# A ring of half batches that two stages of a fused graph kernel share

## The chip, the cores and the metric

The kernel runs on one core of a Trainium2 chip. The metric is the device time of one execution in microseconds, the median of three runs. A profile is one further execution, recorded by the hardware profiler; its span runs from the first to the last instruction. Engines are named as in the profile: PE (matrix products), DVE (vector), ACT (activations), POOL (GpSimd) and SP (here it only issues DMAs; SPq is its queue of issues).

## The reference, cut to what matters

Four graph layers are applied to `x` of 128 batches x 128 nodes x 128 features with an adjacency of 128 x 128 per batch. The second layer is the one that costs:

```python
# layer 1, h is the normed and rectified x
D = jnp.abs(x[:, :, None, :] - x[:, None, :, :])      # every pair of nodes
h = jnp.einsum('bijc,oc->bijo', D, W1) + b1            # 128 -> 64 features per pair
m = jnp.mean(h, axis=(0, 1, 2))                        # over ALL batches and pairs
v = jnp.mean((h - m) ** 2, axis=(0, 1, 2))
h = (h - m) / jnp.sqrt(v + EPS) * g1 + be1
h = _leaky(h)
s = jnp.einsum('bijo,uo->biju', h, W2)[..., 0] + b2[0]
s = jnp.where(A_init > 0, s, NEG)
A = jax.nn.softmax(s, axis=-1)
y = jnp.einsum('bij,bjc->bic', A, x)
y = y @ Wg.T + bg                                      # then a second norm over all batches
```

The mean and the variance `m`, `v` are taken over all batches, so the pair features of every batch have to exist before the first score can be computed. They don't fit on the core: 2 MB for each of 128 batches (pairs are symmetric, so only about half of them are made). A second norm over all batches (`mg`, `vg`) stands before the rest of the layer and the two attention layers that follow.

## The kernel before

It has three stages, cut by the two norms over all batches. The batches go in 32 groups of four (`G = 4`, `NG = 32`).

**First stage** (L261 to L740). For every batch four tiles `t` are made (`NT = 4`), each of 128 x 1024 elements. Per tile: a difference (`d`, L311, on DVE for two tiles and on POOL for two), its absolute value (L352, ACT, three tiles of four), the products with W1 into PSUM (`hp`, L321 and L324, PE), a copy to SBUF (`evacuate`, L335, ACT), and the statistics of the copy (L342, L343, DVE). The copies of one batch stand in one tile `halves[b]` of four parts (`hs`, three buffers, 16 KB per partition each). When the fourth part is there, one DMA of 2 MB writes it to memory, `HP[b]` (L370). Beside this runs the first graph layer of each group (`chain`, L401). The order of all this is set ahead of time: every piece is a `step` with an engine, a cost, the steps it comes after and a rank, and `_ordered` (L115) writes the instructions of each engine in the order of a small plan. SP is one of these engines, so its DMAs stand in one queue, in which a DMA that waits holds those behind it.

**The seam** (L743 to L780). From the statistics `ST1` come, in a few small steps on DVE, PE and POOL in a pool `bn`, the factors `scale1` and `bias1`.

**Second stage** (L783 to L1108). The pair features come back in halves of 1 MB: `fetch(n)` loads the n-th half into a tile `z` (L796), of which there are `FETCHED = 10`. Ten loads are issued ahead; slot `b` then issues two more (L903, L904), into the buffers that batch `b` leaves. A slot (`slot`, L871) does for batch `b + 1` the activation of the first half in place (L878, ACT), the rectified second half into `zr` (L882, ACT) and the leaky maximum of the first (L896, DVE); for batch `b` the products with W2 (`products`, L849: `w2z` with the first half, `w2l` with the second, `w2r` with `zr`); and for batch `b - 1` the copy `su` (L874), the turn into rows `pk` (L860) and the scores `sk` (L867). After each fourth batch a `chain` (L907) is worked through for the group, with its pieces hung into later slots by `at(slot, place, work)`: the scores are written to memory (`rows`, L928), x is loaded (L931), the scores are read back in another order (`u`, L935), then come eight slots of softmax and small products, from `s0 = 4 g + 9` on, up to `y` (L978) and its statistics (`stored`, L980). `x1` and `y` go to memory (L983, L984), but for the last five groups (`KEPT = 5`), which stay on chip in `X1` and `Y`. After the last batch, 12 slots hold only the last groups' chains, and besides them `brief` (L1018), small constants for the third stage, from slot 129 on.

**Third stage** (L1111 to L1400). From the second norm's statistics (`ST2`) come `scale2` and `bias2`; then the rest of the layer and two attention layers per group, planned by `_planned` (L79), with the groups in `Y` first.

Tiles come from pools. A pool that takes memory which another pool has given back lets its first user wait for all that was done in that memory. In the kernel before, the first `fetch` therefore waits for the first stage's buffers and for the pool `bn` of the seam.

Of the kernel before, what the change touches and what calls it, by code (L numbers as in the profile page):

```python
# [17 lines left out]
P = 128  # L18
G = 4
# [149 lines left out]
def tile_gnn_stack(ctx: ExitStack, tc: tile.TileContext, a: dict, out: bass.AP):  # L169
# [5 lines left out]
    res = ctx.enter_context(tc.tile_pool(name="res", bufs=1))  # L175
    small = ctx.enter_context(tc.tile_pool(name="small", bufs=4))
    early = ctx.enter_context(ExitStack())
    psum = early.enter_context(tc.tile_pool(name="psum", bufs=1, space=bass.MemoryType.PSUM))
    banks = {"sm": 2}

# [80 lines left out]
    with tc.tile_pool(name="c0", bufs=1) as c0, tc.tile_pool(name="p0", bufs=2) as p0, ExitStack() as ctx0:  # L261
# [33 lines left out]
        def step(name, engine, cost, after, rank, work, takes=(), gives=()):  # L295
            steps.append((name, engine, cost, after, takes, gives, rank, work))
# [31 lines left out]
        def evacuate(i):  # L328

            b, t = divmod(i, NT)  # L330
            if t == 0:
                halves[b] = p0.tile([P, NT, KC * P], F32, name="hs", bufs=3)
                if b % G == 0:
                    stats[b // G] = p0.tile([P, 2 * NT + 1, G, 6], F32, name="st")
            nc.scalar.copy(halves[b][:, t, :], linear.pop(i))  # L335

        def statistics(i):

            b, t = divmod(i, NT)
            last = t == NT - 1  # L340
            hs, st = halves[b][:, t, :], stats[b // G][:, :, b % G, :]
            nc.vector.bn_stats(st[:, 2 * t, :], hs[:, 0:512])  # L342
            nc.vector.bn_stats(st[:, 2 * t + 1, :], hs[:, 512:1024 - P * last])  # L343
            if last:
                nc.vector.bn_stats(st[:, 2 * NT, :], hs[:, 1024 - P:])
            if last and b % G == G - 1:
                of_all = stats.pop(b // G).rearrange("p a g b -> p a (g b)")
                nc.vector.bn_aggr(ST1[:, b // G, 0, :], of_all[:, 0:2 * NT, :].rearrange("p a b -> p (a b)"))
                nc.vector.bn_aggr(ST1[:, b // G, 1, :], of_all[:, 2 * NT, :])
# [4 lines left out]
        def pairs(i):  # L354

            b, t = divmod(i, NT)
            n, by_max = b // 2, t == BY_MAX
            engine, cost, rank = ("Pool", 4.22, i - 3) if t in ON_POOL else ("DVE", 2.2, i - 2)
            step(("d", i), engine, cost, [("again", n), ("d", i - 2), ("hp", i - 4)], rank, lambda: difference(i))
            if not by_max:  # L360
                step(("abs", i), "ACT", 1.8, [("d", i)], i - 1, lambda: absolute(i))
            step(("hp", i), "PE", 3.44 if by_max else 1.72,
                 [("d" if by_max else "abs", i), ("hp", i - 1), ("hs", i - 2)] + [("xw", n)] * by_max,
                 i, lambda: products(i))
            step(("hs", i), "ACT", 0.9, [("hp", i), ("hs", i - 1)]
                 + [("st", i - 2 * NT - 1), ("out", b - 3)] * (t == 0), i + 1, lambda: evacuate(i))
            step(("st", i), "DVE", (1.3 if b % G < G - 1 else 2.4) if t == NT - 1 else 1.21, [("hs", i), ("st", i - 1)], i + 2,
                 lambda: statistics(i))
            if t == NT - 1:
                step(("out", b), "SP", 0.4, [("hs", i)], i + 1.5, lambda: nc.sync.dma_start(HP[b], halves[b]))  # L370

        def features(g, half):

# [313 lines left out]

        pick = const.tile([P, 2, 8], F32, name="pick")  # L690
        nc.gpsimd.tensor_copy(pick.rearrange("p h (a c) -> p h a c", a=2),
                              ident.rearrange("p (c r) -> p r c", c=4)[:, 0:4, :]
# [12 lines left out]
                chain(g)  # L705
        for i in range(NT * NB):
            pairs(i)
        with tc.manual_schedule():

            b1 = col("b1", a["b1"], 64)  # L710
# [72 lines left out]
    early.close()  # L783
    middle = ctx.enter_context(ExitStack())
    keep = ctx.enter_context(tc.tile_pool(name="keep", bufs=1))
    Y, X1 = ({g: keep.tile([P, G, P], F32, name=f"{n}{g}") for g in range(NG - KEPT, NG)} for n in ("y", "x1"))
    psum = middle.enter_context(tc.tile_pool(name="psum2", bufs=1, space=bass.MemoryType.PSUM))
    banks = {"ps": 3, "pk": 2, "sm": 3}
    with tc.tile_pool(name="c1", bufs=1) as c1, tc.tile_pool(name="p1", bufs=2) as p1:
        fetched, prepared, scored = [], {}, {}  # L790

        def fetch(n):

            if n < 2 * NB:
                z = p1.tile([P, NT // 2 * KC * P], F32, name="z", bufs=FETCHED)
                nc.sync.dma_start(z, HP[n // 2][:, n % 2 * NT // 2:(n % 2 + 1) * NT // 2, :]  # L796
                                  .rearrange("p a b -> p (a b)"))
                fetched.append(z)

        for n in range(FETCHED):  # L800
            fetch(n)


        z0 = c1.tile([P, 1], F32, name="z0")
        nc.vector.scalar_tensor_tensor(z0, bias1, 0.01, bias1, op0=OP.mult, op1=OP.max)
# [36 lines left out]
        def at(slot, place, work):  # L842
            jobs.setdefault((slot, place), []).append(work)
# [60 lines left out]
                fetch(2 * b + FETCHED + 1)  # L904
            now(b, "s")

        def chain(g):  # L907

            rows = slots[g % 2]
            t = {}  # L910
            s0 = G * g + 2 * G + 1

            def four(out, left, right):
                for k in range(G):
# [11 lines left out]
            def to_rows():  # L926
                to = rows[0, 0, 0:1]
                nc.sync.dma_start(bass.AP(tensor=to.tensor, offset=to.offset,  # L928
                                          ap=[[ROW + 1, P], [P * ROW, G], [1, 1 + 2 * KH]]), sk[g % 2])
                t["x"] = p1.tile([P, G, P], F32, name="x", bufs=3)  # L930
                nc.sync.dma_start(t["x"], X[g])  # L931

# [50 lines left out]
                    nc.sync.dma_start(X[g], t["x1"])  # L983
                    nc.sync.dma_start(Z[g], t["y"])  # L984

            at(s0 - 4, "s", to_rows)
            at(s0 - 2, "s", from_rows)
            at(s0, "e", normed)
            at(s0, "p", lambda: turned("pt", t["h"]))
            at(s0, "l", folded)  # L990
# [25 lines left out]
        own_k = const.tile([P, 4], F32, name="own_k")  # L1016

        def brief():  # L1018
            t, end = {}, NB + 1

            def scratch():
                left = p1.tile([P, NT // 2 * KC * P], F32, tag="zr", bufs=3, name="brief")
                for name, n in (("wt0", P), ("wt1", P), ("add_b", 8), ("bounds", 24), ("square", 16), ("bound", 1),
                                ("left", P + 8), ("part", P + 8), ("one0", P + 8), ("one1", P + 8),
                                ("one2", P + 8), ("by_batch", 16)):
                    t[name], left = left[:, 0:n], left[:, n:]
                nc.gpsimd.memset(t["bounds"], 0.0)
                nc.gpsimd.memset(t["part"], 0.0)
                nc.gpsimd.memset(ones3, 1.0)
                nc.vector.tensor_copy(ident_b, ident)  # L1030
                nc.vector.tensor_scalar(no_edge, ident, NEG_EDGE, None, op0=OP.mult)
# [69 lines left out]
            at(end + 8, "l", owners)  # L1101

        with tc.manual_schedule():
            for g in range(NG):
                chain(g)
            brief()
            for b in range(-1, NB + 3 * G + 1):
                slot(b)  # L1108
# [10 lines left out]


    middle.close()
    with tc.If(nc.values_load(bounded, min_val=0, max_val=1) > 0) as cmp, \
            tc.tile_pool(name="p3", bufs=1) as p3, \
            tc.tile_pool(name="ps3", bufs=1, space=bass.MemoryType.PSUM) as ps3:
        pieces = {}
        for heads in (4, 1):
            pieces[heads] = []
# [474 lines left out]
```

## Time and profile before

| | us |
|---|---|
| runs (three) | 2803.29, 2803.65, 2803.67 |
| median | 2803.65 |
| span of the profiled execution | 2798.6 |
| first stage, to the last evacuation | 0 to 1527.6 |
| second stage, ACT's first step of a batch: first and last start | 1539.2, 2286.2 |
| last statistics of y, first step of the third stage | 2335.7, 2339.1 |

How the page is read: its first part gives each engine's busy time and share of the span, the second the span in 40 slices of 70 us with a digit for the busy tenths. Over the whole span PE is busy for 88%, DVE for 88%, ACT for 85%, POOL for 61%. An average over three stages with different limits doesn't say which of them bounds which stage. The groups of instructions that the change touches or leans on, with count, busy time, the mean duration of one in ns, and the engine's idle time before them with what ended it:

```profile
L335 ACT COPY hs<-hp 128x1024 f32<-128x1024 f32 x512 | 516.7, 1028 | 30.7 <-PE hp L324 24.0
L896 DVE SCALAR_TENSOR_TENSOR z<-z 128x2048 f32<-128x2048 f32 x128 | 295.1, 2306 | 21.7 <-ACT z L878 21.7
L878 ACT ACTIVATE z<-z,bias,scale 128x2048 f32<-128x2048 f32 x128 | 267.3, 2088 | 19.0 <-DMA z<-hp 19.0
L882 ACT ACTIVATE zr<-z,bias,scale 128x2048 f32<-128x2048 f32 x128 | 267.4, 2089 | 4.7 <-DMA z<-hp 3.8
...
hp<-hs SPq DMA_DIRECT2D x128, 2048.0 KB, 6.3
z<-hp SPq DMA_DIRECT2D x256, 1024.0 KB, 14.3
u<-rows SPq DMA_DIRECT2D x32, 384.0 KB, 11.4
```

The last three lines are DMA issues: count, size, and the median time from issue to landing. The pair features are 268 MB out and 268 MB back, of 652 MB that the kernel moves in all.

### The profile page before, as it was taken

Reading aid. Unit: us, or ns where it says so; the run is one execution under the profiler, and the core shown is the slowest. Engines: PE = TensorE matmul, PEld = TensorE weight load, DVE = VectorE, ACT = ScalarE, POOL = GpSimd, SP = SyncE. Lnnn points to the kernel's source line nnn. Section 1 sums busy time; section 2 is a strip of 40 time slices with the busy share of each in tenths; the row PEclk is TensorE's granted clock in tenths of the full one; section 3 lists DMA queues with packets and bytes.
Section 4 is the critical chain, followed back from the end, with each engine's and each line's share of the span. In section 5 each row is a group of like instructions: output and inputs, shape, how many; then the busy total and the mean of one; then the engine's idle time right before and its main releaser. Section 6 shows DMA issues by size and latency. Waiting matters only on the chain.

```text
span 2798.6 us, 41745 instructions
## 1 busy us (share of the span) xinstructions
PE 2453.5 (88%) x14521; PEld 1178.8 (42%) x14521; DVE 2474.2 (88%) x4712; ACT 2391.9 (85%) x2837; POOL 1720.2 (61%) x1629
## 2 busy tenths in 40 slices
PE   3899999999999999999997798888888886999986
PEld 2333333333333333333332244444444444777775
DVE  4899999999999999999998588888888886899876
ACT  4799999999999999999997778877878765888975
POOL 6699999999999999999986001111000115555642
PEclk8899999999999999999999899999999998999998
DMA  7454555554555555554545999999999971121110
GB/s 285 169 207 202 204 207 212 213 211 200 207 202 208 207 218 207 207 211 200 207 203 217 418 410 412 411 413 411 411 412 413 413 266 46 46 67 59 58 31 25
DMA packets 179802, 652.40 MB, mean 233 GB/s; under 512 B 30963, under 2 KB 98678, under 8 KB 130422
## 3 DMA queue, kind: packets, MB, share of 16 engines
q1 hardware_dynamic: 179136, 649.39, 58.6%
q8 instruction: 120, 1.97, 0.3%
q14 instruction: 108, 0.88, 0.1%
q10 hardware_dynamic: 438, 0.17, 0.0%
HBM read 337.22 MB, written 312.28 MB: 232 GB/s over the span
## 4 chain that ended last, share of the span: by engine, by line
ACT 35%; PE 22%; DVE 21%; DMA 8%; issue 7%; POOL 5%; SPq 0%; ACTq 0%; DVEq 0%; POOLq 0%
ACT d L352 14%; ACT hs L335 10%; PE hp L321 5%; PE ps L853 5%; DVE z L896 4%; DVE d L311 3%; DMA rows<-sk 3%; POOL d L311 3%; DMA z<-hp 2%; DMA u<-rows 2%; PE hp L324 2%; PE pk L860 2%; ACT h L1206 2%; PE pv L1322 2%; ACT h L493 1%
## 5 line engine op out<-in xcount | busy, mean ns | idle before, releaser
L311 POOL TENSOR_TENSOR d<-xe 128x2048 f32<-128x2048 f32 x256 | 1074.1, 4201 | 59.0 <-PE hp L321 53.8
L321 PE MATMUL hp<-d,w1T 128*64 128x512 f32 x4096 | 997.1, 602 | 123.5 <-ACT hs L335 83.9
L352 ACT ACTIVATE d<-d 128x2048 f32<-128x2048 f32 x384 | 734.4, 1935 | 41.8 <-DVE d L311 22.9
L311 DVE TENSOR_TENSOR d<-xe,xp 128x2048 f32<-128x2048 f32 x256 | 579.4, 2263 | 4.7 <-PE hp L321 2.7
L321 PEld LDWEIGHTS hp<-d,w1T 128*64 128x64 f32 x4096 | 285.4, 137 | 642.1 <-issue 480.6
L335 ACT COPY hs<-hp 128x1024 f32<-128x1024 f32 x512 | 516.7, 1028 | 30.7 <-PE hp L324 24.0
L942 POOL TENSOR_TENSOR x<-x,bt 128x512 f32<-128x512 f32 x32 | 43.8, 1367 | 684.8 <-DMA x<-x 641.3
L342 DVE BATCH_NORM_STATS2 st<-hs 128x6 f32<-128x512 f32 x512 | 349.1, 682 | 43.5 <-ACT hs L335 43.1
L343 DVE BATCH_NORM_STATS2 st<-hs 128x6 f32<-128x512 f32 (+1 forms) x512 | 329.0, 643 | 0.0
L896 DVE SCALAR_TENSOR_TENSOR z<-z 128x2048 f32<-128x2048 f32 x128 | 295.1, 2306 | 21.7 <-ACT z L878 21.7
L878 ACT ACTIVATE z<-z,bias,scale 128x2048 f32<-128x2048 f32 x128 | 267.3, 2088 | 19.0 <-DMA z<-hp 19.0
L882 ACT ACTIVATE zr<-z,bias,scale 128x2048 f32<-128x2048 f32 x128 | 267.4, 2089 | 4.7 <-DMA z<-hp 3.8
L324 PE MATMUL hp<-both_t,xw 128*64 128x512 f32 x1024 | 268.1, 595 | 0.0
L853 PE MATMUL ps<-z,w2z 128*32 128x512 f32 x1024 | 143.8, 634 | 81.6 <-DVE z L896 81.6
L860 PEld LDWEIGHTS pk<-pick,su 128*128 128x128 f32 x1024 | 126.1, 194 | 134.4 <-DVE su L874 88.2
L860 PE MATMUL pk<-pick,su 128*128 128x16 f32 x1024 | 138.5, 267 | 17.6 <-DVE su L874 17.6
L1322 PE MATMUL pv<-wr,e 128*128 128x128 f32 x1024 | 140.5, 283 | 5.9 <-DVE e L1299 4.0
L853 PE MATMUL ps<-z,w2l 128*32 128x512 f32 x1024 | 143.1, 628 | 0.0
L324 PEld LDWEIGHTS hp<-both_t,xw 128*64 128x64 f32 x1024 | 80.7, 138 | 141.2 <-issue 141.2
L853 PE MATMUL ps<-zr,w2r 128*32 128x512 f32 x1024 | 139.9, 619 | 0.0
L1322 PEld LDWEIGHTS pv<-wr,e 128*128 128x128 f32 x1024 | 128.1, 196 | 13.3 <-DVE e L1299 4.1
L1299 DVE SCALAR_TENSOR_TENSOR e<-e,ps 128x512 f32<-128x512 f32 x160 | 106.9, 677 | 26.1 <-ACT ps L1296 25.4
(243 smaller groups left out, 3828.1 us busy)
## 6 DMA issues: line engine op xcount, KB each, us to landing
hp<-hs SPq DMA_DIRECT2D x128, 2048.0 KB, 6.3
z<-hp SPq DMA_DIRECT2D x256, 1024.0 KB, 14.3
x<-x SPq DMA_DIRECT2D x118, 256.0 KB, 11.6
u<-rows SPq DMA_DIRECT2D x32, 384.0 KB, 11.4
x<-in_x_dram SPq DMA_DIRECT2D x32, 256.0 KB, 3.0
adj<-in_adj_dram SPq DMA_DIRECT2D x32, 256.0 KB, 3.3
part<-in_adj_dram SPq DMA_DIRECT2D x16, 512.0 KB, 7.8
out_dram<-x SPq DMA_DIRECT2D x32, 256.0 KB, 2.4
```

Source lines behind the costliest of these rows:

```text
L311: eng.tensor_tensor(d, ahead, x[:, None, None, :].to_broadcast([P, 2, KC, P]), OP.max if t == BY_MAX else OP.subtract)
L321: nc.tensor.matmul(hp[64 * hh:64 * hh + 64, c:c + 512], w1T2 if by_max else w1T, d[:, hh, c:c + 512], start=True, stop=not by_max, skip_gr ...
L324: nc.tensor.matmul(hp[64 * hh:64 * hh + 64, c:c + 512], XW[i // NT // 2][:, i // NT % 2, :], both_t.rearrange("p h k i -> p h (k i)")[:, h ...
L335: nc.scalar.copy(halves[b][:, t, :], linear.pop(i))
L342: nc.vector.bn_stats(st[:, 2 * t, :], hs[:, 0:512])
L343: nc.vector.bn_stats(st[:, 2 * t + 1, :], hs[:, 512:1024 - P * last])
L352: nc.scalar.activation(diffs[i], diffs[i], AF.Abs)
L853: nc.tensor.matmul(ps[32 * c:32 * c + 32, :], w[:, w0:w0 + 32], v[:, 512 * c:512 * c + 512], start=j0 == 0, stop=w is w2r, skip_group_chec ...
L860: nc.tensor.matmul(pk[:, kk, 0:16], su[:, kk, :], pick.rearrange("p h j -> p (h j)"), start=True, stop=True)
L882: nc.scalar.activation(zr, z1, AF.Relu, bias=bias1, scale=scale1[:, 0:1])
L896: nc.vector.scalar_tensor_tensor(z0, z0, 0.01, z0, op0=OP.mult, op1=OP.max)
L1322: nc.tensor.matmul(t[pv][:, k % 2, hd, :], t[e][:, hd, :], flat[:, at:at + P], start=True, stop=True)
```

## The change

One ring of ten half batches (`ring`, tag `z`) now serves both stages; it stands at the right end of SBUF from the first stage to the end of the second.

- In the first stage `evacuate` takes a new half of the ring for every second tile, and `kept(b, half)` writes each half by itself (1 MB) as soon as it is filled. The evacuations come after the statistics and the writes of five batches before, where it was three.
- The last four batches (group 31) are not written. A new step `fetch`, the last in SP's order, appends their eight halves, which are still in the ring, to the list of fetched halves, and loads the two halves of batch 0 into the ring's other two.
- The second stage takes batches in the order 124 to 127, 0 to 123, so its turn 0 is group 31 and turn t is group t - 1. Groups 26 to 30 stay on chip instead of 27 to 31.
- The last turn's `rows` come one slot earlier, its `u` and its eight steps two slots earlier.
- `brief` begins in slot 12 instead of 129, and has its scratch in `selfb` and a tile of its own instead of a `zr`.
- The pools of the second and third stage are made with `reuse_waits="tile"`: a tile then waits for what was done in its own piece of memory.

```diff
         def evacuate(i):
             b, t = divmod(i, NT)
-            if t == 0:
-                halves[b] = p0.tile([P, NT, KC * P], F32, name="hs", bufs=3)
-                if b % G == 0:
-                    stats[b // G] = p0.tile([P, 2 * NT + 1, G, 6], F32, name="st")
-            nc.scalar.copy(halves[b][:, t, :], linear.pop(i))
+            if t % 2 == 0:
+                halves[b, t // 2] = held_z()
+            if t == 0 and b % G == 0:
+                stats[b // G] = p0.tile([P, 2 * NT + 1, G, 6], F32, name="st")
+            nc.scalar.copy(half_of(b, t), linear.pop(i))
+
+        def kept(b, half):
+            to = HP[b][:, half * NT // 2:(half + 1) * NT // 2, :]
+            nc.sync.dma_start(to.rearrange("p a b -> p (a b)"), halves[b, half])
...
             step(("hs", i), "ACT", 0.9, [("hp", i), ("hs", i - 1)]
-                 + [("st", i - 2 * NT - 1), ("out", b - 3)] * (t == 0), i + 1, lambda: evacuate(i))
+                 + [("st", i - 4 * NT), ("out", b - FETCHED // 2)] * (t % 2 == 0), i + 1, lambda: evacuate(i))
...
-            if t == NT - 1:
-                step(("out", b), "SP", 0.4, [("hs", i)], i + 1.5, lambda: nc.sync.dma_start(HP[b], halves[b]))
+            if t == 1 and b < NB - G:
+                step(("out0", b), "SP", 0.4, [("hs", i)], i + 1.5, lambda: kept(b, 0))
+            if t == NT - 1 and b < NB - G:
+                step(("out", b), "SP", 0.4, [("hs", i)], i + 1.5, lambda: kept(b, 1))
...
+        ring = early_ring.enter_context(tc.tile_pool(name="ring", bufs=1, side="right"))
+        fetched = []
+
+        def held_z():
+            return ring.tile([P, NT // 2 * KC * P], F32, tag="z", bufs=FETCHED, name="z")
+
+        def fetch(n):
+            if n < 2 * NB:
+                b, half, z = n // 2 - G, n % 2, held_z()
+                nc.sync.dma_start(z, HP[b][:, half * NT // 2:(half + 1) * NT // 2, :].rearrange("p a b -> p (a b)"))
+                fetched.append(z)
+
+        def first_fetches():
+            fetched.extend(halves[b, half] for b in range(NB - G, NB) for half in range(2))
+            for n in range(2 * G, FETCHED):
+                fetch(n)
...
+        step("fetch", "SP", 0.8, [("hs", NT * NB - 2), ("st", NT * NB - 2 * NT), ("out", NB - G - 1)], NT * NB, first_fetches)
...
-    psum = middle.enter_context(tc.tile_pool(name="psum2", bufs=1, space=bass.MemoryType.PSUM))
+    psum = middle.enter_context(tc.tile_pool(name="psum2", bufs=1, space=bass.MemoryType.PSUM, reuse_waits="tile"))
...
-    with tc.tile_pool(name="c1", bufs=1) as c1, tc.tile_pool(name="p1", bufs=2) as p1:
+    with tc.tile_pool(name="c1", bufs=1, reuse_waits="tile") as c1, \
+            tc.tile_pool(name="p1", bufs=2, reuse_waits="tile") as p1:
...
-        for n in range(FETCHED):
-            fetch(n)
...
-        def chain(g):
-            rows = slots[g % 2]
+        def chain(turn):
+            rows, own_sk = slots[turn % 2], sk[turn % 2]
             t = {}
-            s0 = G * g + 2 * G + 1
+            g = (turn - 1) % NG
+            final = turn == NG - 1
+            s0 = G * turn + 2 * G + 1 - 2 * final
...
-            at(s0 - 4, "s", to_rows)
-            at(s0 - 2, "s", from_rows)
+            at(G * turn + G + 1 - final, "s", to_rows)
+            at(G * turn + G + 3 - 2 * final, "s", from_rows)
...
         def brief():
-            t, end = {}, NB + 1
+            t, end = {}, 3 * G
...
     middle.close()
+    early_ring.close()
     with tc.If(nc.values_load(bounded, min_val=0, max_val=1) > 0) as cmp, \
-            tc.tile_pool(name="p3", bufs=1) as p3, \
-            tc.tile_pool(name="ps3", bufs=1, space=bass.MemoryType.PSUM) as ps3:
+            tc.tile_pool(name="p3", bufs=1, reuse_waits="tile") as p3, \
+            tc.tile_pool(name="ps3", bufs=1, space=bass.MemoryType.PSUM, reuse_waits="tile") as ps3:
```

## The prediction

> **What bounds the kernel now.** I read the page's slices, then the windows of the second stage, then its waits, and last the seams before and after it in the timeline and the chain. From the page and the windows:
>
> ```profile
> DMA  7454555554555555554545999999999971121110
> GB/s 285 169 207 202 204 207 212 213 211 200 207 202 208 207 218 207 207 211 200 207 203 217 418 410 412 411 413 411 411 412 413 413 266 46 46 67 59 58 31 25
> ...
> 1535.00:1560.00 25.00, 15.28 (x105) 5.50 (x108) 13.29 (x21) 17.64 (x9) 0.56 (x1) 0.72 1.00 412
> 1700.00:1800.00 100.00, 87.86 (x686) 42.55 (x686) 85.54 (x132) 80.99 (x56) 10.17 (x8) 1.00 1.02 412
> 2100.00:2200.00 100.00, 88.43 (x674) 41.69 (x670) 85.86 (x130) 80.69 (x58) 10.45 (x8) 0.98 1.03 413
> 2275.00:2300.00 25.00, 22.18 (x175) 10.88 (x168) 22.78 (x37) 15.47 (x12) 4.15 (x7) 1.00 0.36 115
> ```
>
> A window row ends in granted clock, DMA share and GB/s. From 1534 to about 2277 us the DMA engines hold a share of 1.0 and 412 GB/s, in the cold start and in steady state alike, while no engine is above 89%. The first stage moves half of that beside four engines at about 95%; the third moves next to nothing.
>
> Does this rate set the pace? Per group of four batches the DMA issues are 8 halves of 1024 KB, x in, x1 and y out (256 KB each), u (384) and rows (130): 9.70 MB, at 0.412 MB/us 23.5 us. ACT's first step of a batch starts 128 times from 1539.2 to 2286.2: 747.0/127 = 5.88 us a batch, 23.5 a group. They agree. From the waits of the second stage (us in total, times, longest) and the timeline of its start:
>
> ```profile
> DVE u L946 <- DMA u<-rows: 35.4, 25, 2.5
> ...
> 1534.02 39.74 SPq L796 DMA_DIRECT2D z<-hp  x22
> 1535.09 0.48 DVE L780 SCALAR_TENSOR_TENSOR bias<-bias,scale,be 128x1 f32<-128x1 f32 x1
> 1539.22 2.09 ACT L878 ACTIVATE z<-z,bias,scale 128x2048 f32<-128x2048 f32 x1 [11.65 <-DMA z<-hp]
> 1545.40 1.93 PE L853 MATMUL ps<-z,w2l 128*32 128x512 f32 x8
> ```
>
> In steady state ACT never waits for z; the full DMA queue shows in the small u, which lands late behind the large transfers and holds DVE 35.4/27 = 1.3 us a group. Without it a group would take 23.5 - 1.3 = 22.2; the one group that passed as the queue emptied took 22.8 (pz at 2269.96 and 2292.72 in the chain). So engines 22.2 to 22.8, DMA 23.5: DMA bounds the stage by a small margin. In the start, scale and bias are ready at 1535.57, the data 3.65 us later, because the loads were issued only at 1534.02.
>
> The tail, from the chain:
>
> ```profile
> 2305.35 1.71 PE pz L974 x2
> 2318.73 1.87 PE pz L974 x2
> 2332.86 2.09 PE pz L974 x2
> 2338.78 5.20 DMA y<-z
> ```
>
> Here DMA is idle and each of the last groups costs 13.4 to 14.1 us of serial steps.
>
> **What the Trainium skill says.** "DMA: Bandwidth & Descriptors", section Bandwidth, has 425 GB/s for a 16 MB load with one core streaming, under a port ceiling of 435; the trace's 412 is close below, so I take 412 as the most that this stage gets, not a demand that happens to be flat. Its section Anatomy of one DMA (written for another issue path) puts about 2 us of fixed cost on each, so a lone 1 MB load would take some 4.4 us (an estimate from that page); the shortest here took 5.0, the median 14.3: the difference is queueing. "TensorE: Matmul & The Clock Gate", Part 1, says that the clock is halved after an idle window and restored after some 3.4 us of activity; the trace agrees (clock 0.72 in 1535 to 1560, products of 1.93 us and 1.07 us in turn), so the first products of the stage stay slow however early they start.
>
> **The change part by part**, against the profiled execution (span 2798.6; the median of the runs is 2803.65, so 5.05 lie around the span).
>
> 1. *Eight halves are no longer written and read back.* The writes fall in the first stage, beside engines that set its time (DMA share 0.5): nothing. The reads leave the bound of the second: 8 x 1.049 MB / 0.412 = 20.4 us. Two more halves (batch 0) are fetched into the two free slots before the stage starts: 2.10/0.412 = 5.1 us. Together -25.5 us of DMA time.
>
> 2. *The stream starts later.* Before, ten loads went out at 1534.0. Now the ring is full, and the next load waits until the second product of the first batch has read its buffers. Before that was at 1545.40 + 1.93 = 1547.3, 8.1 after ACT's 1539.2. Now ACT waits only for the bias, and starts at about 1535.65; the buffers are free at 1543.8. DMA stands idle from the landing of batch 0 until then: +9.8. From there one pair is asked for per 4.97 us (ACT's pace at 1575.43, 1580.41, 1585.37) and takes 5.1, so the queue doesn't empty. Parts 1 and 2: -15.7, if DMA is the bound to the end. Do the engines keep up? They need (113 batches after the first 15) 22.2 to 22.8 a group against 23.5, and start 3.6 us earlier without the 5.5 us wait of DVE for the first u (1605.1). Yes, with half a microsecond a group to spare.
>
> 3. *The small constants (brief) move from the tail to slots 12 to 20.* Some 26 DVE instructions of 0.13 to 0.34 us, 5.4 us in all, 1.9 on PE, 0.6 on ACT. They stood in DVE's idle time of the tail; now they stand in a loop where DVE is 86% busy. Queued behind them on DVE are z L896 and su L874, and for those PE waits. Nothing if DMA still has a queue then, all 7.9 if everything is in line. The queue is young there (some 5 us built up in slots 0 to 9), so I take +2.
>
> 4. *The last turn is two slots shorter* (rows, u, and its eight steps each earlier). In the tail 12 slots follow the last scores at 3.4 us each (13.6/4), two fewer are -6.8; but two chains now share the slots at a distance of two, and PE at half clock is in line for both. Following DVE and PE step by step from 2309.1 I come to the last statistics at 2330.2 where they were at 2336.4: -6. Bounds 0 (the shared slots grow by as much) and -8.
>
> 5. *The first stage.* The order of the instructions on PE, ACT, DVE and POOL stays as it was; SP issues 248 halves in place of 128 wholes, at 0.3 us each, and has time. The ring is five batches deep where there were three, so no evacuation waits longer. But ACT's copies with a second wait go from 125 to 231: 106 more, each an instruction of 17 ns on a full ACT. Copies behind one start a median of 117 ns before the end of their predecessor, the others 123 ns, so 6 ns each is the low end and 17 ns the high one: I take the low one, +0.6 (up to 1.8).
>
> 6. *Waits by tile.* POOL's cap moves ahead of the scale's root (0.62 us) but waits only for the first stage's end at 1527.6, and the root starts at 1533.97: nothing. In the third stage POOL's constants no longer wait for loads, and what follows them (off until 2346.0, then rs) comes a little earlier: -0.3. The chain would have y's load (5.20 us) there, but six ACT steps run through without a gap beside it, so bounds 0 and -3. PE's first product of the stage now waits on all DMA counters; the latest transfer that it could mean, batch 0, has landed by 1533.
>
> Order of the groups: group 31 comes first and its x1 and y are stored, groups 26 to 30 stay on chip: five as before.
>
> Sum: -15.7 + 2 - 6 + 0.6 - 0.3 = -19.4; span 2779.2, time 2784.2.
>
> **Rivals.**
>
> *Engines pace it.* For: the DMA margin is thin, brief is added, and half-clock spells (2187 and 2259: products of 3.5 us in the chain) make groups of 25. Against: DMA was never short of work. The place where both kernels then differ: before, ACT's 15th start was at 1621.1; now 1535.65 + 10 x 4.97 + 4 x 5.6 = 1607.8, plus 5.4 of brief 1613.2. With 23.5 a group as before the last is at 1613.2 + 28.25 x 23.5 = 2277.1, -9.1; tail and rest -5.7. Time 2788.9.
>
> *Slower: the DMA pause isn't made good.* With a full ring and only two loads ahead, loads follow the engines; if the loop with its young queue loses time at each half-clock spell, and DMA then waits too, a group takes longer than either bound. It decides from 28.25 P = 2286.2 + 5.7 - 1613.2, P = 24.0 us; groups of 24.1 to 25.0 occur before (pz 2173.48 to 2198.26: 24.8). At an average of 24.5 it costs +13.4: 2817. Against: by the starts of u's fold these are five of 28 groups; the rest are near 23.4 with the u wait inside.
>
> *It moves nothing that counts:* the saved bytes turn into idle DMA, and brief and the shared tail slots eat the rest; within 5 us of 2803.
>
> *More:* the third stage's loads did hold its start, and the tail gives its full 8: another -5, 2779.
>
> **How the numbers follow.** Forecast 0.60, engines pace it 0.25, more 0.03, nothing 0.05, slower 0.07. 0.2% is 5.6 us, about what a measurement here can tell from none; the first three are faster: 0.88, within 0.05, slower 0.07. Range: below, the tail at -8, the third stage at -3 and brief at 0 give 2777; above, engines' pace with brief and all 1.8 of part 5, and no gain in the tail, give 2796. 2777 to 2796 leaves the last two cases out.
>
> **What would show it.** The first ACT step of the second stage within 0.2 us of the bias (part 2); no z loads between the two of batch 0 and some 8 us after it, then 412 GB/s to within a few us of the last load; the last load about 15 us earlier after the stage's seam; a u wait that is small at first and returns to 1.3 (DMA bound) or stays at nothing (engines); the last two pz some 7 us apart. Wrong: a DMA share well under 1.0 in mid-stage, groups above 24 us, or a first stage longer by more than 2 us.

## The result and the profile after

| | before | after |
|---|---|---|
| median of the runs (four each) | 2803.66 us | 2775.97 us |
| lowest, highest | 2803.29, 2803.99 | 2774.61, 2781.11 |
| ratio of the times | | 0.9906 (95%: 0.9892 to 0.9921) |

The kernel became 27.7 us faster in the medians. The execution that was profiled is the slowest of the four (2781.11 us, span 2779.3). The two profiles, cut at the same events, in us:

| stretch | before | after | difference |
|---|---|---|---|
| first stage, to its last evacuation | 1527.57 | 1525.56 | -2.0 |
| seam, to ACT's first step of the second stage | 11.65 | 7.70 | -4.0 |
| start, ACT's first step of the 1st to that of the 15th batch | 81.90 | 70.78 | -11.1 |
| middle, the same from the 15th to the 128th batch | 665.03 | 670.88 | +5.9 |
| tail, from the last of these ACT steps to the third stage's bias | 52.84 | 42.60 | -10.2 |
| third stage | 459.56 | 461.80 | +2.2 |
| span | 2798.56 | 2779.31 | -19.25 |

Not all of these rows are the change: the same kernel profiled a second time had 666.4 in the middle and 463.2 in the third stage, and the third stage took 458.8 to 463.5 in all fourteen profiles of this study, of kernels of both kinds. The seam, the start and the tail came out near the first profile's in the second one (7.9, 70.4 and 44.2). Start and middle aren't independent, though: when the engines run ahead in the start and DMA sets the end, the middle gets longer by what the start got shorter. Where it matters they are taken together.

From the page after, the 40 slices of DMA share and rate:

```profile
DMA  7455555555555555555543899999999971121110
GB/s 283 171 223 201 212 201 210 210 212 201 208 201 208 211 209 207 208 207 215 206 193 125 330 409 411 410 411 410 409 410 410 409 266 54 46 69 58 58 31 25
```

Three windows of it (a row has the busy time of PE, PEld, DVE, ACT and POOL and ends in granted clock, DMA share, GB/s):

```profile
1528.00:1545.00 17.00, 9.25 (x52) 3.69 (x52) 10.21 (x29) 11.74 (x6) 0.81 (x2) 0.60 0.25 77
1545.00:1560.00 15.00, 15.00 (x131) 6.64 (x130) 12.58 (x17) 15.00 (x9) 0.00 (x0) 1.00 1.01 411
1700.00:1800.00 100.00, 88.07 (x688) 42.25 (x680) 85.61 (x135) 82.94 (x59) 12.67 (x8) 1.00 1.03 410
```

DMA now has a hole: in slice 22 (1459 to 1529 us, 125 GB/s) the last four batches are no longer written, and in the seam (77 GB/s from 1528 to 1545) the ring is full. It is at its full rate from 1545 on, with PE busy for all of the 15 us from 1545 to 1560, of which it had 12.99 before. The rate that it holds is 410 where it was 412 to 413. The timeline of the start (start, duration, engine, line):

```profile
1533.01 0.22 DVE L809 SCALAR_TENSOR_TENSOR bias<-bias,scale,be 128x1 f32<-128x1 f32 x1
1533.26 2.09 ACT L896 ACTIVATE z<-z,bias,scale 128x2048 f32<-128x2048 f32 x1 [7.70 <-DVE bias L809]
1537.24 2.08 ACT L896 ACTIVATE z<-z,bias,scale 128x2048 f32<-128x2048 f32 x1
1537.73 1.94 PE L871 MATMUL ps<-z,w2z 128*32 128x512 f32 x8 [3.21 <-DVE z L914]
1539.72 5.36 SPq L710 DMA_DIRECT2D z<-hp  x4
1541.21 2.08 ACT L896 ACTIVATE z<-z,bias,scale 128x2048 f32<-128x2048 f32 x1
```

ACT's first step waits for the bias and nothing else, 0.03 us after it is ready. The batches follow at 3.98 us (1533.26, 1537.24, 1541.21), where most came at 4.97 before. The two halves of batch 0 were issued within the first stage, at 1487.07 and 1491.51. The next load goes out at 1539.72, as soon as the product of the first half (1537.73 + 1.94) has read its buffer. From the waits of the second stage (us in total, times, longest):

```profile
DVE u L966 <- DMA u<-rows: 38.1, 24, 5.5
```

The groups of the page that answer to those of before (busy, mean ns, idle before and its cause), and two DMA issues:

```profile
L336 ACT COPY z<-hp 128x1024 f32<-128x1024 f32 x512 | 516.9, 1028 | 47.1 <-PE hp L325 24.4
L914 DVE SCALAR_TENSOR_TENSOR z<-z 128x2048 f32<-128x2048 f32 x128 | 296.6, 2317 | 6.5 <-ACT z L896 6.5
L896 ACT ACTIVATE z<-z,bias,scale 128x2048 f32<-128x2048 f32 x128 | 267.1, 2087 | 9.3 <-DVE bias L809 7.7
...
hp<-z SPq DMA_DIRECT2D x248, 1024.0 KB, 3.9
z<-hp SPq DMA_DIRECT2D x248, 1024.0 KB, 14.2
```

Of ACT's 19.0 us of waiting for z data before this step 1.6 are left. But DVE still waits for u in 24 of 32 turns: 5.5 and 0.4 us in turns 0 and 1, nothing in turns 2 to 5, and 0.7 to 2.6 in turns 6 to 27. The reading is that the large transfers are the limit again from turn 6 on; the runs without the stores and with the last group read back test it below. The tail, from the timeline, the last four groups' products:

```profile
2280.97 1.13 PE L994 MATMUL pz<-yT,wgT 128*128 128x512 f32 x2
2292.62 1.13 PE L994 MATMUL pz<-yT,wgT 128*128 128x512 f32 x2
2307.79 1.13 PE L994 MATMUL pz<-yT,wgT 128*128 128x512 f32 x2 [0.55 <-ACT yT L944]
2312.32 1.13 PE L994 MATMUL pz<-yT,wgT 128*128 128x512 f32 x2 [0.73 <-ACT yT L944]
```

The third of them comes 15.2 us after the second, and the last, whose chain shares slots with it, only 4.5 us later; before, the steps were 12.6, 13.4 and 14.1.

### The profile page after: what moved, and what is told of

Its sections match the earlier page's. It is cut to its first block, busy times and chain, and to the rows that moved or that the text cites. A ratio compares the mean times of both kernels' runs of the same rounds, so it can differ in the third digit from the quotient of the medians.

```text
span 2779.3 us, 42065 instructions
## 1 busy us (share of the span) xinstructions
PE 2457.4 (88%) x14521; PEld 1182.0 (43%) x14521; DVE 2472.0 (89%) x4712; ACT 2388.7 (86%) x2837; POOL 1724.0 (62%) x1629
## 4 chain that ended last, share of the span: by engine, by line
ACT 33%; PE 22%; DVE 19%; issue 11%; DMA 10%; POOL 3%; SPq 1%; ACTq 0%; DVEq 0%; POOLq 0%
ACT d L360 11%; ACT z L336 11%; PE hp L322 6%; PE ps L871 5%; DMA rows<-sk 4%; DVE d L312 3%; DMA u<-rows 3%; DVE z L914 3%; DMA z<-hp 3%; PE hp L325 2%; ACT h L1229 2%; PE pk L878 2%; PE pv L1345 2%; ACT o L462 1%; ACT h L503 1%
## 5 line engine op out<-in xcount | busy, mean ns | idle before, releaser
L336 ACT COPY z<-hp 128x1024 f32<-128x1024 f32 x512 | 516.9, 1028 | 47.1 <-PE hp L325 24.4
L962 POOL TENSOR_TENSOR x<-x,bt 128x512 f32<-128x512 f32 x32 | 46.5, 1455 | 672.1 <-DMA x<-x 629.0
L350 DVE BATCH_NORM_STATS2 st<-z 128x6 f32<-128x512 f32 x512 | 349.3, 682 | 42.4 <-ACT z L336 42.1
L351 DVE BATCH_NORM_STATS2 st<-z 128x6 f32<-128x512 f32 (+1 forms) x512 | 329.3, 643 | 0.0
## 6 DMA issues: line engine op xcount, KB each, us to landing
z<-hp SPq DMA_DIRECT2D x248, 1024.0 KB, 14.2
```

What stands on the lines that cost most here:

```text
L336: nc.scalar.copy(half_of(b, t), linear.pop(i))
```

## The experiments

Unless said otherwise each is an edit of the changed kernel. Times are medians; ratios are to the kernel before on the same chip. Since the changed kernel's own runs lie between 2773.2 and 2781.1 us, differences of 1 to 2 us are read from the stretches of the traces and not from the medians.

### One part of the change undone

**The last group written and read back (reload).** The ring, the early brief, the short turn and the waits stay. The batches come in the order 0 to 127 again, the ten first loads come behind the first stage's last write in SP's order, and groups 27 to 31 stay on chip.

```diff
-            if t == 1 and b < NB - G:
+            if t == 1:
...
-            if t == NT - 1 and b < NB - G:
+            if t == NT - 1:
...
-                b, half, z = n // 2 - G, n % 2, held_z()
+                b, half, z = n // 2, n % 2, held_z()
...
-            fetched.extend(halves[b, half] for b in range(NB - G, NB) for half in range(2))
-            for n in range(2 * G, FETCHED):
+            for n in range(FETCHED):
...
-            g = (turn - 1) % NG
+            g = turn
```

> The changed kernel (ring, waits, early brief, short last turn) with the last group written and read back like the others, in the order 0 to 127, ten loads issued as the ring's halves come free. Theory, DMA bounds the stage: the eight halves come back, 10 loads x 1.049 MB / 0.41 = 25.6 us instead of 2 hidden ones, but the stream starts at about 1527 rather than 1540 to 1545 and has no idle, which gives back 13 to 16: 10 to 12 us slower than the changed kernel, 2786 to 2788, with u waits of about 1.4 us from the first turns on. Rival, engines pace the stage and the early start is all: 0 to 3 us slower, 2776 to 2779. Third: keeping the halves carries the whole of parts 1 and 2: 16 us, 2792.

2787.92 us, ratio 0.9948 (0.9935 to 0.9962): 12.0 us slower than the changed kernel (10.1 beside its second set of runs), as the DMA theory has it. The difference sits in one stretch: the start takes 82.4 us (70.8 in the changed kernel), seam, middle and tail are the same to 0.5 us (7.9, 666.3, 43.7; second profile of the changed kernel 7.9, 666.4, 44.2). Windows of this kernel:

```profile
1525.00:1545.00 20.00, 10.21 (x64) 4.46 (x64) 10.32 (x32) 10.47 (x5) 0.81 (x2) 0.66 1.01 399
1545.00:1600.00 55.00, 38.62 (x284) 16.03 (x284) 33.78 (x43) 44.37 (x22) 2.37 (x5) 0.88 1.02 415
1700.00:1800.00 100.00, 86.94 (x676) 41.76 (x674) 88.07 (x134) 79.02 (x54) 13.22 (x10) 1.00 1.03 410
```

ACT in its timeline:

```profile
1545.03 2.09 ACT L899 ACTIVATE zr<-z,bias,scale 128x2048 f32<-128x2048 f32 x1 [0.40 <-DMA z<-hp]
1547.58 2.09 ACT L895 ACTIVATE z<-z,bias,scale 128x2048 f32<-128x2048 f32 x1 [0.46 <-DMA z<-hp]
1550.10 2.10 ACT L899 ACTIVATE zr<-z,bias,scale 128x2048 f32<-128x2048 f32 x1 [0.43 <-DMA z<-hp]
```

Its loads flow through the seam at 399 GB/s and ACT starts at the bias, and still each ACT step waits 0.4 us for its half: 5 us a batch, DMA's own pace. Starting early isn't what brought the gain of the start; the halves that need no DMA are. Its rate in the middle is 410 GB/s too, below the 412 of before, so the lower rate doesn't come from keeping the last group.

**Brief back in the tail (late_brief).**

```diff
-            t, end = {}, 3 * G
+            t, end = {}, NB + 1
```

> The changed kernel with brief put back into the tail (from slot NB + 1 on); its new scratch stays. By the prediction (part 3) brief cost 2 us in slots 12 to 20 (bounds 0 and 7.9), so without it there the last ACT step of the second stage comes up to 2 us earlier, and in the tail it stands in idle time of DVE: 2774, 2 less than the changed kernel's 2776. Rival: the stage is bound by DMA again by then, so brief's place in the loop costs nothing, and in a tail that is now two slots shorter its 5.4 us of DVE are in line with two chains: the tail from the last ACT step to the bias (42.6) grows by 2 to 5 us, 2778 to 2781.

2778.67 us, 0.9909 (0.9893 to 0.9924). From the last evacuation to ACT's last step 745.5 us, where six kernels with that stretch unchanged have 744.6 to 749.4 (the changed kernel's two profiles: 749.4, 744.7); the tail 43.5, where others with the short turn have 42.5 to 44.2 (one 46.5). Neither is moved: brief costs nothing in the loop, and in the tail nothing that shows. The median, 2.7 us above one set of runs of the changed kernel and 0.9 above the other (2777.82), doesn't tell.

**The last turn at full length (full_tail).**

```diff
-            final = turn == NG - 1
+            final = 0
```

> The changed kernel with the last turn at its regular slots. By the prediction (part 4) the two slots were worth 6 us: 2782, and the tail from the last ACT step to the bias goes from 42.6 to 48.6. Rival: all of the tail's measured shortening (52.8 to 42.6) is due to it: 2786, tail 52.8. Third: the shortening came mostly from brief's leaving the tail and from where half-clock spells fell, and the shorter turn gives 3 or less: 2779.

2781.57 us, 0.9926 (0.9912 to 0.994): 5.6 us slower than the changed kernel (3.8 beside its second set of runs). The tail is 50.5, some 7 above the others. That is near the prediction's 6, not the whole of 10.2.

**Waits by pool (by_pool).** `reuse_waits="tile"` is taken out of the five pools.

> The changed kernel with the default waits in the pools of the second and third stage; the ring stays. By the prediction (part 6) the waits by tile are worth 0.3 us (0 to 3): 2776.3, first ACT step still at the bias, third stage as long as it was. Rival: they carry part of the gain, since small tiles of the second stage (w2r, w2l, own) and y's loads of the third would wait for whole pools: 2 to 5 us, 2778 to 2781, half at the seam, half at the start of the third stage, where y's load would again be in the chain.

2776.42 us, 0.9905 (0.989 to 0.992): no difference. The seam is 8.4 where the changed kernel's two profiles have 7.7 and 7.9, so half a microsecond there; the third stage takes 462.8, within the spread.

### One part alone, in the kernel before

**The shorter last turn (before_tail).**

```diff
-            s0 = G * g + 2 * G + 1
+            final = g == NG - 1
+            s0 = G * g + 2 * G + 1 - 2 * final
...
-            at(s0 - 4, "s", to_rows)
-            at(s0 - 2, "s", from_rows)
+            at(G * g + G + 1 - final, "s", to_rows)
+            at(G * g + G + 3 - 2 * final, "s", from_rows)
```

> The kernel before with the shorter last turn alone (rows one slot, u and its eight steps two slots earlier). Theory: the shorter turn is worth by itself what it was worth in the changed kernel (5.6 us of time, tail 50.5 against 43.5 to 44.2): the tail from the last ACT step to the bias goes from 52.8 to about 46, 2797. Rival: with brief still in the tail the two chains and brief share slots, and it gives 3 or less, 2800. The trace also samples the first stage of the kernel before a second time: the changed kernels end it between 1522.0 and 1525.6, the kernel before at 1527.6. If that is chance, this one ends it between 1522 and 1526; if the ring made the first stage faster, at 1527 or later.

2793.32 us, 0.9966 (0.9952 to 0.9979). The tail goes from 52.8 to 46.8, -6.0. The first stage ended at 1526.6, later than in any ring kernel then known.

**Waits by tile (before_tile).** The same argument in the five pools of the kernel before.

> The kernel before with waits by tile in the pools of the second and third stage, nothing else. Theory: the ten first loads then no longer wait for the seam's small pool and go out at about 1528 after the first stage's end instead of 1534, the stage is bound by DMA from its first load on, so its end comes 4 to 6 us earlier: 2798 to 2800, first ACT step at the bias. Rival: the loads still wait until the last statistics, since their memory is the first stage's: 0 to 1 us, 2803.

2800.13 us, 0.999 (0.9984 to 0.9997): about 2.5 us, between the two. The loads go out at 1529.27, 0.4 us after the last evacuation, where that had been 6.5; ACT starts 10.1 us after it instead of 11.7, and still waits 2.1 us for its data. Of the 6 us by which the loads are earlier less than half arrives at the end.

### What bounds the middle

**Without the stores of x1 and y (no_store).** The kernel leaves out 54 stores of 262 KB, 14.2 MB. Its third stage loads what stands in memory in place of x1, and again in place of y, so its results are not those of the reference; the number and size of the loads stay.

```diff
-                if g not in Y:
+                if g not in Y and False:
...
-                step("lz", "SP", 0.4, (), lambda: load("y", Z[g]))
+                step("lz", "SP", 0.4, (), lambda: load("y", X[g]))
```

> The changed kernel without the stores of x1 and y of the 27 groups that don't stay on chip; the third stage loads for both what memory has in place of x1. Left out: 54 stores of 262 KB, 14.2 MB, 1.28 us of a group's 23.6 at 0.41 MB per us. If DMA bounds the stage, 27 x 1.28 = 34.5 us go until the engines bound it: their pace by the prediction is 22.2 to 22.8 a group, so 0.9 to 1.3 of each group and 23 to 34 in all, 2742 to 2753, u waits near nothing in most turns. If the engines bound it and the share of 1.0 is chance, 0 to 5 us, 2771 to 2776.

2743.78 us (2742.2 to 2760.6 in five runs), 0.9803 (0.9779 to 0.9826): 32.2 us less than the changed kernel. The middle is 636.2 in place of 666.4, -30.2, and 13 groups in a row take 22.3 us each. A window of this kernel:

```profile
1700.00:1800.00 100.00, 91.50 (x713) 43.99 (x712) 86.83 (x136) 84.25 (x61) 15.04 (x9) 1.00 1.02 408
```

Its waits for u from 1610 to 2240 us:

```profile
DVE u L966 <- DMA u<-rows: 16.8, 17, 2.2
```

DMA is still at its full rate: (9.70 - 0.52) MB / 0.408 = 22.5 us a group. The 14.2 MB are 34.5 us at 0.41 MB per us, so most of the bytes that went came off the time. From turn 5 to turn 11 DVE doesn't wait for u at all, and the turns follow each other at 22.3 us: that is the engines' own pace, at the low end of the prediction's 22.2 to 22.8.

**x of three turns loaded in the seam (early_x).** The loads of turns 0 to 2 move from `to_rows` to slot -1.

```diff
+                if turn > 2:
+                    load_x()
+
+            def load_x():
                 t["x"] = p1.tile([P, G, P], F32, name="x", bufs=3)
                 nc.sync.dma_start(t["x"], X[g])
+
+            if turn <= 2:
+                at(-1, "s", load_x)
```

> The changed kernel with the x loads of turns 0 to 2 (three of 262 KB, into buffers that are free anyway) issued right after batch 0's halves, in the seam where DMA stands idle. Theory, DMA bounds the stage from the 16th batch to the end: 0.79 MB / 0.41 = 1.9 us less, 2774. Rival: the start phase is paced by engines and the DMA queue is only filled later, so nothing comes off: 2776.

2776.53 us, 0.9902 (0.9887 to 0.9917): nothing gained, of 1.9 us expected. Two things in the trace are large enough to account for it. In the seam the bias comes 8.9 us after the last evacuation, where it was 7.7 and 7.9: POOL, its x there early, runs an addition beside DVE's small multiplication. And in the middle DMA ran short once, after PE had spent 13.7 us at half clock from 1648.9 on. The seam in the timeline:

```profile
1531.49 1.26 POOL L969 TENSOR_TENSOR x<-x,bt 128x512 f32<-128x512 f32 x1
1531.56 1.21 DVE L805 TENSOR_TENSOR scale<-scale,g 128x1 f32<-128x1 f32 x1 [1.01 <-POOL scale L226]
```

The windows around the spell:

```profile
1650.00:1660.00 10.00, 9.16 (x41) 4.19 (x40) 8.30 (x18) 6.55 (x4) 0.00 (x0) 0.50 1.03 415
1660.00:1680.00 20.00, 17.96 (x133) 8.42 (x136) 14.34 (x23) 14.85 (x11) 1.89 (x2) 0.94 0.98 350
```

L805 takes 1.21 us, in the changed kernel 0.16. And 20 us at 350 instead of 411 GB/s are 3 us of DMA lost. An explanation that isn't tested: the loads follow the engines, and when those are late the queue runs dry.

**The same with turn 0 one slot later (lead).**

```diff
-            s0 = G * turn + 2 * G + 1 - 2 * final
+            s0 = G * turn + 2 * G + 1 - 2 * final + (turn == 0)
```

> The changed kernel with x of turns 0 to 2 loaded in the seam (as in the run before, which gained nothing: after a half-clock spell of 13.7 us its DMA ran short for 2.8 us) and the eight steps of turn 0 one slot later, so that DVE doesn't wait 5.5 to 7.6 us for the first u. Theory: the engines' lead over DMA after the start is what absorbs such spells; with the wait gone the lead grows and the 1.9 us of the x loads come through: 2773 to 2774. Rival: the stage's end is set by DMA from about turn 6 on whatever the lead, and its rate, not its start, is what varies: 2775 to 2777.

2773.76 us, 0.99 (0.9885 to 0.9915), beside the changed kernel's 2777.82, 0.9911 (0.9898 to 0.9925), in the same set: the intervals overlap. The start shrinks to 63.2, and the middle grows to 672.3: together 735.4, with the changed kernel at 736.8. What the engines gain in the start they lose in the middle: their lead is worth next to nothing, DMA sets the end. It is the lowest median of the study, but not shown to beat the changed kernel.

### The rest

**A second profile of the changed kernel (after_again).**

> The changed kernel unchanged, a second profile of it. Its first profile had a second stage 4 us longer (670.9 from the 15th to the last ACT step) than five kernels with the same steady state (666.3 to 667.3). If that was chance (half-clock spells up to 10.2 us), this one has 666 to 667.5 and a time of 2774 to 2777; if it belongs to the kernel, 670 again.

2777.82 us, 0.9911 (0.9898 to 0.9925). The middle is 666.4: the first profile's 670.9 was chance.

**The last turn three slots shorter (short3).** `- 2 * final` in `s0` becomes `- 3 * final`.

> The changed kernel with the last turn's eight steps three slots earlier in place of two (u's load stays where it is, one slot ahead). If slots are what the tail costs, another 3 us: tail from the last ACT step to the bias 40 in place of 42.5 to 44.2, 2773. Rival: the tail is now bound by the serial steps of the two chains and by u's load (2.4 us and its fold behind it), and nothing moves: 0 to 1 us, 2775 to 2776.

2776.97 us, 0.9913 (0.9899 to 0.9926). Tail 43.3: nothing moves, as its rival had it. The last two products are 2.8 us apart in place of 4.5, but the first of them comes 35.3 us after ACT's last step where it came after 32.9 and 34.4: the closer the two chains stand, the later the first of them ends.

**Both halves of a batch written together (late_writes).**

```diff
-            if t == 1 and b < NB - G:
+            if t == NT - 1 and b < NB - G:
                 step(("out0", b), "SP", 0.4, [("hs", i)], i + 1.5, lambda: kept(b, 0))
```

> The changed kernel with both halves of a batch written when the second is filled, one behind the other: 2 MB at once, as before; the ring stays five batches deep. The first stage ended at 1526.6 to 1528.8 in three kernels with the old writes and at 1522.0 to 1525.6 in seven with the ring, 3.9 us apart in the mean, 2.7 of which sit in one place: DVE waiting 2.7 us for an x load at 287 us. Theory: that load stood behind a 2 MB write in the DMA queue, and the halves gave it room; then the wait is back here and the first stage ends at 1526 to 1528, time 2778 to 2780. Rival: the depth of the ring did it (evacuations no longer wait for the write of three batches before); then the wait stays away and the first stage ends at 1522 to 1525.6, 2776.

2776.41 us, 0.9907 (0.9892 to 0.9923); first stage to 1525.2, no wait. But this doesn't decide: the trace shows the two writes around that place at 274.49 and some 5.6 us later, at the same distances as in the changed kernel (from 275.30). In the changed kernel the two writes follow each other at this place already, with nothing between them on SP, and each waits only for the filling of its own half, so the edit moved nothing here. The test didn't make what it was meant to make.

## Why the prediction was right, and where not

The forecast was faster, 2784.2 (2777.0 to 2796.0); it is faster, 2775.97, 1.0 below the low end. The likeliest case is the one that happened: DMA bounds the second stage, the bytes saved are what counts. Its terms:

*Parts 1 and 2 (bytes and later stream, -15.7), part 3 (brief, +2).* From the last evacuation to ACT's last step the kernel before and the one with its tail shortened take 758.6 and 757.0; the ring kernels with this stretch unchanged 744.6 to 749.4, median 745.4: -12.4, against -13.7. Brief's +2 doesn't show: nothing moved when brief went back to the tail, so DMA seems to cover it. The terms of the stream come out of the traces, from the first load after the last evacuation to the landing of the last z:

| | before | changed, both profiles |
|---|---|---|
| first load after the last evacuation | 6.5 us | 14.2, 14.4 us |
| from there to the last landing | 748.8 us | 729.1, 728.2 us |
| moved in that time | 307.0 MB | 296.5 MB |
| rate | 410 GB/s | 407 GB/s |

The 10.5 MB less are worth the 25.5 us that I put. The later stream costs 7.8 and not 9.8: the first free buffer came 14.2 us after the last evacuation where I had 16.2, as a half is free after its own product. And a term stands there that I didn't have: at the lower rate 296.5 MB take some 5 to 6 us longer. Together about -12. Half a per cent of the rate is lost in all of the middle (1640 to 2240 us: 412 GB/s in the three kernels without the ring, 410 in the second profile, and also with the last group read back, with waits by pool, with a full last turn and with brief late). So it goes with none of these parts; the ring itself, which all of these kernels share, is what is left of the change, and why it should slow DMA stays open. One more detail failed: the start's 4.97 us a batch, which I took for ACT's pace, was DMA's (two halves in 5.1), so that with its data on chip ACT went on at 3.98.

*Part 4 (shorter last turn, -6).* Right: -6.0 alone in the kernel before, some -6 to -8 in the changed one. The tail is some 9 us shorter in all (52.7 to 52.8 before, mostly 42.5 to 44.2 after). The 2.3 us between 52.8 and the changed kernel's full tail of 50.5 I can't assign; the run with brief back in the tail doesn't show them there. The products came 4.5 apart and not 7: the chain before the last is stretched in the shared slots, as feared, and the last follows sooner.

*Part 5 (first stage, +0.6).* Wrong in sign, and the step that failed worst. I priced 106 second waits and took it that nothing else moves, "no evacuation waits longer". The second waits cost nothing that shows: from the evacuation of tile 112 to the last one all fourteen kernels take 1127.5 to 1128.0 us. But the first stage ends at 1526.6, 1527.6 and 1528.8 in the three kernels with whole writes and at 1522.0 to 1525.6 in ten with the ring (an eleventh, lead, at 1527.0), 3.3 us apart in the mean. The difference sits in two places. Between the evacuations of tiles 20 and 40 the three take 52.7 us and the eleven 51.6. Between 40 and 112 a spell of half clock on PE (3.4 us) falls into some executions of both kinds: with it the stretch takes 212.8 us with whole writes and 210.1 to 210.2 with the ring, without it 211.4 and 208.7 to 208.9. So the ring saves 1.1 and some 2.6 us there. What comes before tile 20 (133.4 to 137.2 us) varies in both kinds. There the term fails in the other direction too: in all eleven ring kernels the first evacuation does wait longer, 13.2 to 15.5 us for a load of constants, and starts at 69.5 to 72.1 us where it started at 56.0 to 57.3. By tile 20 the means of the two kinds are only 0.4 us apart (135.1 and 135.5); what causes this wait wasn't tested. Before (timeline around 280 us), then after:

```profile
278.97 0.32 SPq L370 DMA_DIRECT2D hp<-hs  x1
280.51 0.38 SPq L418 DMA_DIRECT2D x<-in_x_dram  x1
287.37 0.87 DVE L429 BATCH_NORM_STATS2 lnst<-x 128x6 f32<-128x128 f32 x4 [2.72 <-DMA x<-in_x_dram]
```

```profile
275.30 5.91 SPq L343 DMA_DIRECT2D hp<-z  x2
282.44 0.38 SPq L428 DMA_DIRECT2D x<-in_x_dram  x1
286.50 0.85 DVE L439 BATCH_NORM_STATS2 lnst<-x 128x6 f32<-128x128 f32 x4
```

Before, a load of x goes out 1.5 us behind the 2 MB of batch 17, and DVE waits 2.72 us for it. After, the first half of the same batch leaves at 275.30 and the second 5.6 us later, so that only 1 MB goes ahead of x, and the same statistics start without a wait. The load of adj right behind it lands 7.2 us after its issue before and 4.0 after. The DVE wait is in all three traces of kernels with whole writes and in none of the eleven with the ring; a wait of POOL for adj (1.9 us at 150.7) falls to 0.8 or less. These two waits have the place and about the size of the two differences. Was it the halves or the deeper ring? In the three kernels with whole writes no evacuation waited for a write: L335 was idle for PE alone (24.0 us behind L324 in the page, the rest behind L321). The deeper ring had no such wait to remove, which speaks for the halves; no run separates the two.

*Part 6 (waits by tile, -0.3).* Right in size: 0.5 in the seam, nothing that shows in the third stage. Its first load of y goes out at 2294.27, 23 us ahead of the bias, where before it went out at 2335.08, 4 us ahead of it; but the third stage is no shorter, so these loads weren't what held it.

*The base.* I put 5.05 us around the span. The runs show 1.8 (2781.11 against 2779.3): the profiled execution of before was itself some 3 us shorter than its runs. That the span was forecast as 2779.2 and measured as 2779.31 is luck: the gain in the first stage that I missed, the tail's extra and a slow middle in that one profile cancel.

*The rivals.* Engines as the pace: in the start, yes, and there it is the gain; in the middle no. "Slower" shows in small: DMA ran short by 3 us in one profile and fell to 398 GB/s in 2200 to 2250 of the first one, but it is worth a few us, not 33; in the first of these the rate is back at 413 after 20 us. The sum of what the traces give: first stage -3.3, seam to last ACT step -12.4, tail -9, third stage 0: -25, beside -27.7 and, in the second set of runs, -23.2 of the medians (2800.97 to 2777.82).

## What to carry to other kernels

Where one stage is bound by DMA and the one before it leaves its last results on chip anyway, let the second take those first: their bytes are worth their full DMA time, and the order is free if the reduction between the stages needs all of the data either way. Price the later start of the loads with it: here it took back 7.8 of 25.5 us, and a slightly lower rate 5 to 6 more. Before pricing any other edit in such a stage, ask whether it moves bytes: added engine work and a longer lead of the engines came to nothing here. And count who stands behind a large write in the same queue: a small load waited there for 2.7 us, and with the write cut in two it no longer did.

## What the runs showed of the hardware

- A multiplication of 128 x 1 on DVE took 1.21 us beside an addition of 128 x 512 on POOL that had begun 0.07 us earlier, 0.16 without it, in both kernels where the two met. The Trainium skill, "SBUF — State Buffer", section "SBUF: two separate sides", says that the port pair which DVE and GpSimd share is an exclusive lock, held for the whole instruction; the trace agrees, the DVE instruction ends 0.02 us after the POOL one.
- PE's half-clock spells all but vanish without the stores. Between 1600 and 2235 us the changed kernel spent 47.8 and 27.3 us at half clock in its two profiles, in spells of 3.4 to 10.2 us; without the stores, where DVE waits for u half as much (16.8 us in place of 32.5 between about 1610 and 2250), it was one spell of 3.4. The Trainium skill, "TensorE: Matmul & The Clock Gate", Part 1, has the clock fall after an idle window of about 3.4 us; the lengths agree (multiples of 3.4), but the longest gap of PE in that stretch of the first profile was 2.4 us. The waits for u alone don't explain the spells either: the second profile has more of them (38.4 us) and less half clock. The cause stays open. In the first stage one spell of 3.4 us between tiles 40 and 112 made that stretch 1.4 us longer, in kernels of both kinds.
- One core's DMA held 412 to 413 GB/s before and 409 to 411 after, in every 100 us from 1700 to 2200, with 1 MB loads and transfers of 130 to 384 KB mixed. With the stores left out it was 407 to 409.
